# Two gated cross-attention layers: the first layer's maxima in twelve visits of 500 keys in place of sixteen of 375

## Chip, core and metric

The kernel runs on one core of a Trainium2 chip. The metric is the device time of one launch in microseconds (us). A core has five engines with a queue of instructions each, worked off in order: TensorE (PE in the profile, with its weight loads shown as PEld), VectorE (DVE), ScalarE (ACT), GpSimd (POOL) and SyncE (SP), which issues the DMAs here. They wait for each other by semaphores alone. Matmuls write to PSUM, eight banks of 512 fp32 numbers on each partition; DVE and ACT read it.

## What is computed

Eight sequences of 224 rows and 512 columns pass through two layers. Each layer is a cross-attention over 750 context rows and a feed-forward part, each gated by a tanh and added to its input. Layer 0 has 16 heads of 32 numbers, and its feed-forward part quantizes rows and weights and has a convolution of three taps; layer 1 has 8 heads of 64 and an fp4-quantized feed-forward part.

```python
def _L0_xattn_ref(query, key, value, Wq, Wk, Wv, Wo):
    q, k, v = proj(query, Wq), proj(key, Wk), proj(value, Wv)   # 16 heads x 32
    scores = jnp.einsum('bhqd,bhkd->bhqk', q, k) / jnp.sqrt(jnp.float32(DIM_K))
    attn = jax.nn.softmax(scores, axis=-1)
    x = jnp.einsum('bhqk,bhkd->bhqd', attn, v)
    return x.transpose(0, 2, 1, 3).reshape(b, -1, e) @ Wo.T
...
x = x + jnp.tanh(g_xattn[0]) * _L0_xattn_ref(_layernorm(x, axis=-1), ctx_1024, ctx_1024, ...)
x = x + jnp.tanh(g_ffn[0]) * _L0_ffn_ref(_layernorm(x, axis=-1), ...)
x = x + jnp.tanh(g_xattn[1]) * _L1_xattn_ref(_layernorm(x, axis=-1), ctx_1024, mask, ...)
x = x + jnp.tanh(g_ffn[1]) * _L1_ffn_ref(_layernorm(x, axis=-1), ...)
```

## The kernel before

`run` goes through sixteen attentions: n = 0 to 7 are the eight sequences of layer 0 (`attention16`), n = 8 to 15 those of layer 1 (`attention8`). Then comes layer 1's feed-forward part. The change touches `attention16` alone.

`attention16` has two stages. **The first stage finds the maxima.** For each group g of four heads, each tile i of 112 queries and each half c of 375 keys there is one slot, sixteen in all. A slot has four score matmuls (L504), one for each head, on 32 rows of the array each, into two PSUM tiles `sc` of two banks each; the pool `pair` has two such tiles, so the scores of a slot need the exponentials of the slot before to be done. Two DVE reductions (L512) take the negated maxima of two heads each, and four ACT exponentials (L521) read the same scores with these maxima as bias. Their output `shown` is not used; what counts is the sum (`accum_out`). **The second stage makes the products.** Twelve steps, each for a group and two tiles of 125 keys: the maxima are put into the scores by a small matmul (`pick`, L468), the scores are made transposed (L477), exponentiated by two ACT instructions (L620), and multiplied by the values one step later (`products`, L595). Between the stages `stat_rows` (L446, L450, L456) makes the maxima into rows.

In the rest of the time PE does other work, taken in pieces from generators. `fill(us, ...)` emits pieces until that much PE time is used up, `pace(us, ...)` until DVE is that far behind by the kernel's own count (`self.behind`), and `finish` empties a queue. Emission order is the order on every engine. The pieces are: keys of the next sequence (`keys`, L314, four matmuls of 375 columns for a group), its queries (`queries`: statistics L174, rows L184, transposes L196 with copy L197, matmuls L343), values (`value_tile`, L372, four matmuls of 512 columns, for this layer and for layer 1 later), the output product of the sequence before (`project_out`, L417, with its sum on DVE, L428), and layer 0's feed-forward part, called `ffn0`, with its output product `ffn0_out` (L1040).

Three things matter for the order:

- Keys, queries, values and `project_out` use the PSUM pool `m` of two banks, in turn. A bank is free again when it has been copied out: keys (L323), values (L381) and transposed rows (L197) on ACT, `project_out` on DVE. The copies are emitted after the exponentials of their slot, and ACT keeps that order.
- The `ffn0` of sequence n-1 runs beside attention n (`beside`). What is left of it at the end becomes `old`, and is finished in the first slots of attention n+1 (from n = 2 on). Its last part puts a scale in all partitions (`spread`, matmuls L212, copy L215), then quantizes in four pieces (L1026, L1029); `ffn0_out` takes these four pieces, first for the first tile of rows and then for the second.
- `soon`, `early` and `late` are the queues that `fill` takes from: the first values and `project_out`; `ffn0_out` and the other values; keys and queries of the next sequence. `late` goes on in the second stage.

A slot's two calls of `fill` ask for 1.9 and for 1.6 us plus at most 0.5:

Of the kernel before, what the change touches and what calls it, by code (L numbers as in the profile page):

```python
# [27 lines left out]
F32 = mybir.dt.float32  # L28
# [3 lines left out]
AF = mybir.ActivationFunctionType  # L32
ALU = mybir.AluOpType
AX = mybir.AxisListType

B, S, D = 8, 224, 512
M = 750
TP = 112
TF = 128
NF = B * S // TF  # L40
NT = S // TP
KC = D // 128
MH = M // 2
CP = 125
NKT = M // CP
SOON = 4
# [18 lines left out]
class Net:  # L65
# [31 lines left out]
    def setup(self):  # L97
# [207 lines left out]
    def keys(self, n, c, g):  # L305

        nc, job = self.nc, self.jobs[n]
        if "kT" not in job:
            job["kT"] = [
                self.att.tile([128, M], F32, name="kT", bufs=2 * KC) for _ in range(KC)  # L310
            ]
        pk = self.ps("m", [128, MH])
        for k in range(KC):
# [171 lines left out]
    def attention16(self, n, before, ahead, old, soon, early, late, beside):  # L485

        nc, pool, job = self.nc, self.att, self.jobs[n]
        kT, qT = job["kT"], job["qT"]
        rows = [slice(h * 32, (h + 1) * 32) for h in range(4)]


        part = pool.tile([TP, 2, NT, KC, 4], F32, name="part")
        sums = pool.tile([TP, 2, NT, KC, 4], F32, name="sums")
        slots = KC * NT * 2
        self.behind = 1.0
        for slot in range(slots):  # L500
            g, i, c = slot // (2 * NT), slot // 2 % NT, slot % 2
            sc = [self.ps("pair", [TP, 2, 512]) for _ in range(2)]
            for h, r in enumerate(rows):
                nc.tensor.matmul(  # L504
                    sc[h // 2][:, h % 2, :MH],
                    lhsT=qT[r, g, i * TP : (i + 1) * TP],
                    rhs=kT[g][r, c * MH : (c + 1) * MH],
                    start=True,
                    stop=True,
                )  # L510
            for k in range(2):
                nc.vector.tensor_reduce(  # L512
                    part[:, c, i, g, 2 * k : 2 * k + 2], sc[k][:, :, :MH], AX.X, ALU.max, negate=True
                )
            if slot == 0:
                self.finish([before])

                shown = pool.tile([CP, 4, 2 * S], F32, name="p", bufs=2)
            self.put_off()
            for h in range(4):  # L520
                nc.scalar.activation(  # L521
                    shown[:TP, h, :MH],
                    sc[h // 2][:, h % 2, :MH],
                    AF.Exp,
                    bias=part[:, c, i, g, h : h + 1],
                    accum_out=sums[:, c, i, g, h : h + 1],
                )


            self.fill(1.9, soon, early, late)  # L530
            if slot == 3:
                self.finish(soon)
                self.finish(old)
            elif slot < 3:
                self.pace(1.0, old)
            if slot in (10, 11):

                self.behind += next(ahead)[1]
            if (slot > 2 or n == 0) and slot < slots - 1:
                self.pace(1.0, beside)  # L540
            more = min(max(self.behind - 2.3, 0), 0.5)
            self.fill(1.6 + more, soon, early, late)
            self.behind = max(self.behind - 2.3 - more, 0)
        val = pool.tile([TP, NT, KC, 4], F32, name="val")
        nc.vector.tensor_tensor(val, part[:, 0], part[:, 1], ALU.min)
        transposed = self.stat_rows(self.stat[0][n % 2], val.rearrange("p t g h -> p t h g"))
        self.pace(1.0, beside)
        self.fill(1.3, early, late)
        self.finish(early)
        sT = transposed()  # L550
        self.fill(0.7, late)
        self.behind = max(self.behind - 2.5, 0)

        def divisors():

            less = pool.tile([TP, 2, NT, KC, 4], F32, name="less")
            for c in range(2):
                nc.vector.tensor_tensor(less[:, c], val, part[:, c], ALU.subtract)
            nc.scalar.activation(less, less, AF.Exp)
            self.behind += 0.4  # L560
            yield
            nc.vector.tensor_tensor(sums, sums, less, ALU.mult)
            total = pool.tile([TP, NT, KC, 4], F32, name="total0")
            nc.vector.tensor_tensor(total, sums[:, 0], sums[:, 1], ALU.add)
            nc.vector.reciprocal(total, total)
            transposed = self.stat_rows(self.stat_inv, total.rearrange("p t g h -> p t h g"))
            self.behind += 2.2
            yield
            iT = transposed()
            yield  # L570
            for pair in range(2):
                pi = self.ps("t", [128, 2, S])
                for k in range(2):
                    nc.tensor.matmul(
                        pi[:, k, :],
                        lhsT=self.spread_q[:, 2 * pair + k, :],
                        rhs=iT,
                        start=True,
                        stop=True,
                    )  # L580
                across[pair] = pool.tile([128, 2, S], F32, name="inv")
                nc.scalar.copy(across[pair], pi)
                yield

        aT = job["aT"] = pool.tile([128, KC, S], F32, name="aT")
        more, across, banks = divisors(), {}, {}

        def products(g, j0, p):

            if g % 2 == 0 and j0 == 0:  # L590
                banks["pa"] = self.ps("pa", [128, 2, S])
            for j in (j0, j0 + 1):
                for h, r in enumerate(rows):
                    col = g * 128 + h * 32
                    nc.tensor.matmul(  # L595
                        banks["pa"][r, g % 2, :],
                        lhsT=job["v"][j][:, col : col + 32],
                        rhs=p[:, h, (j - j0) * S : (j - j0 + 1) * S],
                        start=j == 0,
                        stop=j == NKT - 1,  # L600
                    )
            if g % 2 and j0 + 2 == NKT:
                nc.vector.tensor_tensor(
                    aT[:, g - 1 : g + 1, :], banks["pa"], across[g // 2], ALU.mult
                )
                self.behind += 0.6

        last = None
        for step in range(KC * NKT // 2):
            g, j0 = divmod(2 * step, NKT)  # L610
            pw = [self.ps("pair", [CP, 2, 512]) for _ in range(2)]
            k = kT[g][:, j0 * CP : (j0 + 2) * CP]
            self.weights_minus_max(
                [(pw[h // 2][:, h % 2, : 2 * S], r, g, qT[:, g, :], k) for h, r in enumerate(rows)],
                self.pick, sT, True,
            )
            p = pool.tile([CP, 4, 2 * S], F32, name="p", bufs=2)
            self.put_off()
            for k in range(2):
                nc.scalar.activation(p[:, 2 * k : 2 * k + 2, :], pw[k][:, :, : 2 * S], AF.Exp)  # L620
# [12 lines left out]
        def rest():  # L633
            products(*last)
            yield 0.8, 0.6

        return rest()
# [939 lines left out]
```

## Time and profile before

| what | us |
|---|---|
| median of three runs (2120.82 to 2123.0) | 2121.07 |
| the profiled execution | 2120.87 |
| its span on the core | 2119.1 |
| PE busy | 2078.0 (98% of the span) |
| DVE busy | 1362.2 (64%) |
| ACT busy | 1005.9 (47%) |
| maxima of sequence 5: first scores at 667.91, second stage from 749.77 | 81.86 |
| second stage of sequence 5: to the next first scores at 798.48 | 48.71 |

The span is that of the core's instructions; 1.8 us of the execution lie outside it. Busy time counts an instruction from its start to its end, and matmuls overlap, so PE can be short of its full pace while it is counted as busy. In a timeline, neighbouring instructions of one line are merged into one row: start, duration, engine, line, operation, tiles, count, and in brackets the engine's idle time just before with what ended it. An fp32 matmul shows as two matmuls.

### The profile page before, as it was taken

The page shows a single profiled execution, that of the slowest core. Times are in us where ns is not written, and L with a number is a line of the kernel's source. Part 1 is how long each engine was busy: PE and PEld are TensorE (multiplying, and loading weights), DVE is VectorE, ACT ScalarE, POOL GpSimd, SP SyncE. Part 2 cuts the span into 40 slices and gives each one's busy share as a digit, 9 for nine tenths or more (in the row PEclk, how much of TensorE's full clock was granted, in tenths as well). Part 3 has the DMA queues.
Part 4 walks back from the last instruction along what each step waited for, and adds up shares of the span by engine and source line. Part 5 has one row for each costly group of instructions (what it writes and reads, how often), then busy time and mean ns, then how long its engine had stood idle before and what let it go on. Part 6 is the DMA issues. An engine that isn't in the chain of part 4 may idle for free.

```text
span 2119.1 us, 32277 instructions
## 1 busy us (share of the span) xinstructions
PE 2078.0 (98%) x12606; PEld 1197.8 (57%) x12606; DVE 1362.2 (64%) x2795; ACT 1005.9 (47%) x2332; POOL 130.3 (6%) x146
## 2 busy tenths in 40 slices
PE   9999999999999999999999999999999999999999
PEld 5454544545445454554657567667666665565555
DVE  3777666575666756657547667767743577676665
ACT  3656656566565665657626444544544321111111
POOL 0000000000000000000000011111100011111111
PEclk9999999999999999999999999999999999999999
DMA  7301001020010201112021122222320020000000
GB/s 249 99 31 44 6 24 44 1 60 7 28 40 1 66 2 32 35 41 67 25 63 38 47 90 62 93 65 69 112 62 19 28 89 11 5 21 20 20 6 20
DMA packets 58536, 97.63 MB, mean 46 GB/s; under 512 B 3664, under 2 KB 30032, under 8 KB 58256
## 3 DMA queue, kind: packets, MB, share of 16 engines
q1 hardware_dynamic: 58384, 95.57, 14.3%
q8 instruction: 100, 1.64, 0.3%
q14 instruction: 52, 0.43, 0.1%
HBM read 73.47 MB, written 22.09 MB: 45 GB/s over the span
## 4 chain that ended last, share of the span: by engine, by line
PE 94%; ACT 3%; DVE 2%; issue 0%; POOL 0%; ACTq 0%; POOLq 0%; DVEq 0%
PE ps_m L372 16%; PE ps_m L314 15%; PE ps_big L1187 11%; PE ps_m L1219 6%; PE ps_m L417 5%; PE ps_pair L504 5%; PE ps_m L343 5%; PE ps_half L722 4%; PE ps_half L782 4%; PE ps_pa L685 4%; PE ps_pair L477 3%; PE ps_pa L595 3%; PE ps_t L926 2%; PE ps_m L1187 2%; ACT p L620 2%; PE ps_pair L468 2%
## 5 line engine op out<-in xcount | busy, mean ns | idle before, releaser
L521 ACT ACTIVATE p<-ps_pair,part 112x375 f32<-112x375 f32 x512 | 286.2, 571 | 204.3 <-DVE part L512 204.3
L314 PE MATMUL ps_m<-cx,wk 128*128 128x375 f32 x1024 | 367.1, 490 | 12.9 <-ACT xnT L197 11.7
L512 DVE TENSOR_REDUCE part<-ps_pair 112x2 f32<-112x750 f32 x256 | 228.3, 933 | 157.0 <-PE ps_pair L504 157.0
L314 PEld LDWEIGHTS ps_m<-cx,wk 128*128 128x128 f32 x1024 | 181.7, 191 | 123.2 <-issue 22.3
L739 DVE CUSTOM_DVE_ANT_0 ps_half<-ps_half,mbias 112x750 f32<-112x750 f32 x128 | 121.1, 946 | 138.4 <-PE ps_half L722 138.4
L620 ACT ACTIVATE p<-ps_pair 125x896 f32<-125x896 f32 x192 | 165.3, 912 | 90.9 <-PE ps_pair L477 90.2
L372 PE MATMUL ps_m<-wv_later,cx 128*125 128x512 f32 x384 | 185.7, 607 | 0.0
L372 PE MATMUL ps_m<-wv,cx 128*125 128x512 f32 x384 | 182.8, 606 | 0.0
L760 ACT ACTIVATE p<-ps_half,nm 112x750 f32<-112x750 f32 x128 | 113.4, 890 | 67.2 <-DVE nm L751 66.9
L1219 PE MATMUL ps_m<-wd,hqT 128*128 128x512 f32 x308 | 136.6, 592 | 0.0
L504 PE MATMUL ps_pair<-kT,qT 32*112 32x375 f32 x1024 | 122.1, 519 | 0.2
L1198 ACT ACTIVATE gth<-ps_big 128x352 f32<-128x352 f32 x48 | 22.2, 463 | 207.2 <-PE ps_big L1187 198.5
L417 PE MATMUL ps_m<-wo,aT 128*112 128x512 f32 x256 | 118.9, 599 | 0.0
L954 DVE SCALAR_TENSOR_TENSOR y<-hp,cw,y 128x224 f32<-128x224 f32 x256 | 109.5, 449 | 6.5 <-ACT y L940 2.0
L372 PEld LDWEIGHTS ps_m<-wv,cx 128*125 128x125 f32 x384 | 66.4, 187 | 82.0 <-issue 80.6
L343 PE MATMUL ps_m<-xnT,wq 128*128 128x224 f32 x512 | 111.5, 359 | 0.6 <-ACT xnT L197 0.6
L1187 PE MATMUL ps_big<-wu,xqT 128*128 128x352 f32 x352 | 111.3, 459 | 0.0
L1187 PE MATMUL ps_big<-wg,xqT 128*128 128x352 f32 x352 | 111.3, 459 | 0.0
L934 DVE TENSOR_TENSOR hp<-ps_t,bc 128x448 f32<-128x448 f32 x64 | 39.9, 623 | 108.8 <-PE ps_t L926 98.1
L787 ACT COPY p<-ps_half 125x672 f32<-125x672 f32 x128 | 85.8, 722 | 49.8 <-PE ps_half L782 49.7
L372 PEld LDWEIGHTS ps_m<-wv_later,cx 128*125 128x125 f32 x384 | 64.7, 187 | 69.3 <-issue 68.5
L521 ACT ACTIVATION_READ_ACCUMULATOR p<-ps_pair,part 112x1 f32 x512 | 103.7, 203 | 0.0
(226 smaller groups left out, 3168.0 us busy)
## 6 DMA issues: line engine op xcount, KB each, us to landing
cx<-in_ctx SPq DMA_DIRECT2D x32, 750.0 KB
wst<-in_w SPq DMA_DIRECT2D x16, 512.0 KB
v_later<-vsome SPq DMA_DIRECT2D x32, 250.0 KB
v<-v_later SPq DMA_DIRECT2D x32, 250.0 KB
x<-in_x SPq DMA_DIRECT2D x8, 448.0 KB
mid<-x SPq DMA_DIRECT2D x8, 448.0 KB
x<-mid SPq DMA_DIRECT2D x8, 448.0 KB
last<-x SPq DMA_DIRECT2D x8, 448.0 KB
```

The costliest lines, as they stand in the source:

```text
L314: nc.tensor.matmul(pk, lhsT=self.w["wk"][:, k, g * 128 : (g + 1) * 128], rhs=job["cx"][c][:, k, :], start=k == 0, stop=k == KC - 1,)
L343: nc.tensor.matmul(pq[:, g - g0, :], lhsT=self.w["wq"][:, k, g * 128 : (g + 1) * 128], rhs=xnT[:, k, :], start=k == 0, stop=k == KC - 1,)
L372: self.nc.tensor.matmul(pv, lhsT=self.jobs[n]["cx"][c][:, k, at : at + CP], rhs=self.w[weight][:, k, :], start=k == 0, stop=k == KC - 1,)
L417: nc.tensor.matmul(po, lhsT=aT[:, g, i * TP : (i + 1) * TP], rhs=self.w["wo"][:, g, :], start=g == 0, stop=g == KC - 1,)
L504: nc.tensor.matmul(sc[h // 2][:, h % 2, :MH], lhsT=qT[r, g, i * TP : (i + 1) * TP], rhs=kT[g][r, c * MH : (c + 1) * MH], start=True, stop= ...
L512: nc.vector.tensor_reduce(part[:, c, i, g, 2 * k : 2 * k + 2], sc[k][:, :, :MH], AX.X, ALU.max, negate=True)
L521: nc.scalar.activation(shown[:TP, h, :MH], sc[h // 2][:, h % 2, :MH], AF.Exp, bias=part[:, c, i, g, h : h + 1], accum_out=sums[:, c, i, g, ...
L620: nc.scalar.activation(p[:, 2 * k : 2 * k + 2, :], pw[k][:, :, : 2 * S], AF.Exp)
L739: nc.vector.tensor_tensor_reduce(out=src, in0=src, in1=masks[i], scale=1.0, scalar=-MASKED, op0=ALU.add, op1=ALU.max, accum_out=mx,)
L760: nc.scalar.activation(p[:, h, :].rearrange("p (c k) -> p c k", c=2), sc[h][:, :, :MH], AF.Exp, bias=nms[h], accum_out=total[:, i, h, g : ...
L1187: nc.tensor.matmul(ps[:, :CW], lhsT=xqT[:, k, :], rhs=wt[:, k, c0 : c0 + CW], start=k == 0, stop=k == KC - 1,)
L1219: nc.tensor.matmul(po, lhsT=hqT[:, k, :], rhs=wd[:, k, :], start=k == 0, stop=k == NC1 - 1)
```

## The change

Each group of heads now has three slots in place of four. The first slot takes keys 0 to 499 for query tile 0. The second takes keys 500 to 749 for tile 0 and keys 0 to 249 for tile 1, side by side in one PSUM bank. The third takes keys 250 to 749 for tile 1. So every slot fills 500 columns of a bank. The middle one has eight score matmuls of 250 columns and eight exponentials of 250; the others have four of 500 each. A slot still has two reductions, over 1000 numbers on each partition in place of 750, and in the middle slot one reduction gives four maxima. `shown` is now one row of 500 numbers that all heads write. `part` and `sums` have their axes in another order, and `val`, `less` and `total0` follow it. With twelve slots the calls between them have other sizes and places: `fill` asks for 1.9 and then 2.5 (middle slot: 3.7) plus at most 0.5, `old` gets `pace(2.0)` in slot 0 and is finished in slot 1 (before: `pace(1.0)` in slots 0 to 2, finished in slot 3), `soon` is finished from slot 2 on, and `beside` gets `pace(1.4)` from slot 2 to 10 (before: 1.0 from slot 4 to 14).

```diff
+WIDE = 500
...
-        part = pool.tile([TP, 2, NT, KC, 4], F32, name="part")
-        sums = pool.tile([TP, 2, NT, KC, 4], F32, name="sums")
-        slots = KC * NT * 2
+        part = pool.tile([TP, NT, 2, KC, 4], F32, name="part")
+        sums = pool.tile([TP, NT, 2, KC, 4], F32, name="sums")
+        parts = part.rearrange("p i c g h -> p (i c) g h")
+        added = sums.rearrange("p i c g h -> p (i c) g h")
+        pieces = (
+            ((0, 0, WIDE),),
+            ((0, WIDE, M), (1, 0, M - WIDE)),
+            ((1, M - WIDE, M),),
+        )
+        slots = KC * len(pieces)
         self.behind = 1.0
         for slot in range(slots):
-            g, i, c = slot // (2 * NT), slot // 2 % NT, slot % 2
+            g, third = divmod(slot, len(pieces))
+            some = pieces[third]
+            width = some[0][2] - some[0][1]
+            two = len(some) == 2
             sc = [self.ps("pair", [TP, 2, 512]) for _ in range(2)]
-            for h, r in enumerate(rows):
-                nc.tensor.matmul(
-                    sc[h // 2][:, h % 2, :MH],
-                    lhsT=qT[r, g, i * TP : (i + 1) * TP],
-                    rhs=kT[g][r, c * MH : (c + 1) * MH],
-                    start=True,
-                    stop=True,
-                )
+            for e, (i, k0, k1) in enumerate(some):
+                for h, r in enumerate(rows):
+                    nc.tensor.matmul(
+                        sc[h // 2][:, h % 2, e * width : (e + 1) * width],
+                        lhsT=qT[r, g, i * TP : (i + 1) * TP],
+                        rhs=kT[g][r, k0:k1],
+                        start=True,
+                        stop=True,
+                    )
+            ats = slice(third + (third == 2), third + (third == 2) + len(some))
             for k in range(2):
                 nc.vector.tensor_reduce(
-                    part[:, c, i, g, 2 * k : 2 * k + 2], sc[k][:, :, :MH], AX.X, ALU.max, negate=True
+                    parts[:, ats, g, 2 * k : 2 * k + 2].rearrange("p e h -> p h e"),
+                    sc[k][:, :, :WIDE].rearrange("p h (e w) -> p h e w", w=width),
+                    AX.X,
+                    ALU.max,
+                    negate=True,
                 )
...
             for h in range(4):
-                nc.scalar.activation(
-                    shown[:TP, h, :MH],
-                    sc[h // 2][:, h % 2, :MH],
-                    AF.Exp,
-                    bias=part[:, c, i, g, h : h + 1],
-                    accum_out=sums[:, c, i, g, h : h + 1],
-                )
+                for e in range(len(some)):
+                    at = ats.start + e
+                    nc.scalar.activation(
+                        shown[:, e * width : (e + 1) * width],
+                        sc[h // 2][:, h % 2, e * width : (e + 1) * width],
+                        AF.Exp,
+                        bias=parts[:, at, g, h : h + 1],
+                        accum_out=added[:, at, g, h : h + 1],
+                    )
             self.fill(1.9, soon, early, late)
-            if slot == 3:
+            if slot == 1:
+                self.finish(old)
+            elif slot == 0:
+                self.pace(2.0, old)
+            else:
                 self.finish(soon)
-                self.finish(old)
-            elif slot < 3:
-                self.pace(1.0, old)
-            if slot in (10, 11):
+            if slot in (7, 8):
                 self.behind += next(ahead)[1]
-            if (slot > 2 or n == 0) and slot < slots - 1:
-                self.pace(1.0, beside)
-            more = min(max(self.behind - 2.3, 0), 0.5)
-            self.fill(1.6 + more, soon, early, late)
-            self.behind = max(self.behind - 2.3 - more, 0)
+            if (slot > 1 or n == 0) and slot < slots - 1:
+                self.pace(1.4, beside)
+            free = 3.6 if two else 2.6
+            more = min(max(self.behind - free, 0), 0.5)
+            self.fill((3.7 if two else 2.5) + more, soon, early, late)
+            self.behind = max(self.behind - free - more, 0)
```

More of the change, by code (lines that the diff above doesn't have):

```diff
@@ L518, in attention16 @@
                 shown = pool.tile([CP, 4, 2 * S], F32, name="p", bufs=2)
+                shown = shown[:TP].rearrange("p h q -> p (h q)")[:, :WIDE]
             self.put_off()
             for h in range(4):
-                nc.scalar.activation(
-                    shown[:TP, h, :MH],
-                    sc[h // 2][:, h % 2, :MH],
-                    AF.Exp,
-                    bias=part[:, c, i, g, h : h + 1],
-                    accum_out=sums[:, c, i, g, h : h + 1],
-                )
-            self.fill(1.9, soon, early, late)
-            if slot == 3:
+                for e in range(len(some)):
[7 more added lines that the diff above has]
+                    )
+            self.fill(1.9, soon, early, late)
+            if slot == 1:
[3 more added lines that the diff above has]
+            else:
                 self.finish(soon)
-                self.finish(old)
-            elif slot < 3:
-                self.pace(1.0, old)
-            if slot in (10, 11):
+            if slot in (7, 8):
                 self.behind += next(ahead)[1]
-            if (slot > 2 or n == 0) and slot < slots - 1:
-                self.pace(1.0, beside)
-            more = min(max(self.behind - 2.3, 0), 0.5)
-            self.fill(1.6 + more, soon, early, late)
-            self.behind = max(self.behind - 2.3 - more, 0)
+            if (slot > 1 or n == 0) and slot < slots - 1:
[4 more added lines that the diff above has]
+            self.behind = max(self.behind - free - more, 0)
         val = pool.tile([TP, NT, KC, 4], F32, name="val")
-        nc.vector.tensor_tensor(val, part[:, 0], part[:, 1], ALU.min)
+        nc.vector.tensor_tensor(val, part[:, :, 0], part[:, :, 1], ALU.min)
         transposed = self.stat_rows(self.stat[0][n % 2], val.rearrange("p t g h -> p t h g"))
@@ L554, in divisors @@
         def divisors():
-            less = pool.tile([TP, 2, NT, KC, 4], F32, name="less")
+            less = pool.tile([TP, NT, 2, KC, 4], F32, name="less")
             for c in range(2):
-                nc.vector.tensor_tensor(less[:, c], val, part[:, c], ALU.subtract)
+                nc.vector.tensor_tensor(less[:, :, c], val, part[:, :, c], ALU.subtract)
             nc.scalar.activation(less, less, AF.Exp)
@@ L563, in divisors @@
             total = pool.tile([TP, NT, KC, 4], F32, name="total0")
-            nc.vector.tensor_tensor(total, sums[:, 0], sums[:, 1], ALU.add)
+            nc.vector.tensor_tensor(total, sums[:, :, 0], sums[:, :, 1], ALU.add)
             nc.vector.reciprocal(total, total)
```

## The prediction

> **What bounds the kernel now.** I read the page first, then the waits, then the timelines of sequence 5 (start, last slot), of the end of sequence 0, and the clock.
>
> ```profile
> PE 2078.0 (98%) x12606; PEld 1197.8 (57%) x12606; DVE 1362.2 (64%) x2795; ACT 1005.9 (47%) x2332; POOL 130.3 (6%) x146
> ...
> L521 ACT ACTIVATE p<-ps_pair,part 112x375 f32<-112x375 f32 x512 | 286.2, 571 | 204.3 <-DVE part L512 204.3
> ...
> L512 DVE TENSOR_REDUCE part<-ps_pair 112x2 f32<-112x750 f32 x256 | 228.3, 933 | 157.0 <-PE ps_pair L504 157.0
> ```
>
> PE sets the time. The reductions are a large group on DVE, but DVE is idle for 36% of the span, so a microsecond saved there is none saved in the end.
>
> ```profile
> 430.15 0.90 PE L504 MATMUL ps_pair<-kT,qT 32*112 32x375 f32 x8
> 430.98 0.29 PEld L372 LDWEIGHTS ps_m<-wv,cx 128*125 128x125 f32 x2 [0.54 <-issue]
> 430.98 3.70 PE L372 MATMUL ps_m<-wv,cx 128*125 128x512 f32 x8
> 431.08 1.78 DVE L512 TENSOR_REDUCE part<-ps_pair 112x2 f32<-112x750 f32 x2 [1.79 <-PE ps_pair L504]
> 431.51 0.19 PEld L372 LDWEIGHTS ps_m<-wv,cx 128*125 128x125 f32 x1 [0.24 <-issue]
> 431.94 0.19 PEld L372 LDWEIGHTS ps_m<-wv,cx 128*125 128x125 f32 x1 [0.24 <-issue]
> ...
> 432.12 0.57 ACT L521 ACTIVATE p<-ps_pair,part 112x375 f32<-112x375 f32 x1 [2.08 <-DVE part L512]
> ...
> 432.68 0.56 ACT L521 ACTIVATE p<-ps_pair,part 112x375 f32<-112x375 f32 x1
> ...
> 434.23 0.21 ACT L521 ACTIVATION_READ_ACCUMULATOR p<-ps_pair,part 112x1 f32 x1
> ```
>
> Rows are start, duration, engine, line. This is one slot of sequence 3. PE goes on with a value tile while the slot's chain runs: scores to reduction 0.93, reduction to first exponential 1.04, exponentials every 0.555, free at 434.44, 4.29 after the scores began. PE's own slot is 4.46. So the chain is hidden by 0.17.
>
> ```profile
> 744.65 0.54 ACT L197 COPY xnT<-ps_m 128x448 f32<-128x448 f32 x1
> ...
> 745.25 0.58 PE L314 MATMUL ps_m<-cx,wk 128*128 128x375 f32 x1 [2.06 <-ACT xnT L197]
> ```
> ```profile
> PE ps_m L314 <- ACT xnT L197: 11.7, 6, 2.1
> ```
>
> The wait that does reach PE: a copy that frees a bank of `m` stands behind the slot's exponentials on ACT. It costs 2.06 in each of six sequences.
>
> ```profile
> 145.88 1.73 ACT L620 ACTIVATE p<-ps_pair 125x896 f32<-125x896 f32 x2 [1.19 <-PE ps_pair L477]
> ...
> 146.85 1.69 PE L504 MATMUL ps_pair<-kT,qT 32*112 32x375 f32 x8
> ```
> ```profile
> 614.30:617.70 3.40, 3.40 (x13) 1.92 (x12) 1.05 (x3) 0.00 (x0) 0.00 (x0) 0.50 0.00 0
> ```
>
> The first shows steps without fill: ACT's two exponentials set the pace (steps start every 2.91), and the next scores take 1.69 in place of 0.90. The second: 0.50 is the granted clock, for 3.4 us after a wait of 2.06.
>
> **The change, part by part.**
>
> *A. Scores on PE: -12.3.* Passes of 512 columns start every 0.43, so a column costs 0.84 ns. A slot's eight matmuls run as two passes (four row tiles at once): 2 x 375 x 0.84 = 0.63. The slot takes 0.83 until the next line starts, 0.09 more before it (last pass of L372 to the scores) and 0.10 in the first pass after it (430.98 to 431.51 in place of 0.43): 1.02, of which 0.39 is entry and exit. A slot of 500 columns is 0.84 + 0.39 = 1.23; the middle slot has four passes of 250, also 0.84, and enters once. Per sequence 16 x 1.02 = 16.3 becomes 12 x 1.23 = 14.8. Eight times 1.53 is 12.3. If each query tile in the middle slot paid entry again (3 x 0.09 over 32 slots = 8.6), 3.7 is left. I take 12.3: the second stage's L477 passes of 224 columns follow each other at 0.19 on the same row tiles.
>
> *B. DVE and ACT: nothing by themselves.* 64 reductions fewer, each with some 0.15 fixed (750 numbers 0.93, L819's 1024 in 1.21, 1.04 ns each), save DVE 9.6, hidden by its idle time; if DVE were the bound that would be the gain. ACT has as many exponentials as before: 256 of 500, 256 of 250. By the rows of 375 (0.571) and 750 (L760, 0.890) they take 0.85 ns a column, so one comes every 0.66 or 0.45. A slot's chain is then 0.93 + 0.21 (two passes, 125 columns more), 1.29 (1000 numbers: 1.19), and 2.8 or 3.75: free 5.2 after the scores began, 6.2 in the middle slot. PE's slot with fill of 4.4 or 5.6 takes 5.6 or 6.8, so the chain itself is still hidden, now by 0.4 to 0.6. Small DVE operations with other strides cost the same.
>
> The Trainium skill ("Perfetto Trace Analysis", Optimizing Scalar/DVE Operations) says grouping helps where the engine is saturated, and where it is not but makes bubbles elsewhere, instructions should be broken up. The rule speaks against this change. By it the sum would be a loss too; it gives no size.
>
> *C. Fill moves out of the second stage: +16.1.* In the built program's order, sequence 5 has 66.4 of fill in the maxima (before 61.7), and 17.1 in the products (21.8). The last three steps have 0.63, 0 and 0.22, where before had 1.7 to 2.0. A filled step takes 2.18 plus its fill (647.62 to 651.32: 3.70 with 1.51). An empty one takes 2.91: +0.73. After an empty last step the next scores wait 0.8 (1.69 in place of 0.90). Sequences 3 to 6: 0.1 + 0.73 + 0.5 + 0.8 = 2.1 each, 8.5. Sequence 7: 1.3. Sequence 0 gets four more empty steps, 2.9; sequence 1 three at part price, 1.6; sequence 2 1.0 + 0.8. (Those after 0 and 1 wait already.) If DVE work kept such steps slow anyway, half: 8; DVE running out of time too (L970 takes 1.73): 20.
>
> *D. `old` in slot 1: +14.0.* In sequences 4 to 7 the whole end of `ffn0` now falls into slot 1. The copy L215 stands behind the eight exponentials: from the slot's scores 6.2, copy 0.36, then four times 1.08 + 0.63 on DVE (rows L1026, L1029), the first ready at 8.3. PE reaches `ffn0_out` after 1.23 + 1.72 + 0.3 + 3.43 = 6.7 and waits 1.6. In slot 2 it waits 0.4 and 0.85 for pieces three and four. Slot 2's reductions are behind all this and L428 on DVE; its exponentials end 0.35 after PE is done: 3.2 a sequence, 12.8. Sequence 3 has L215 earlier, and waits 0.85 + 0.35: 1.2. Before, half of these pieces ran in the last steps and the rest in two slots. If this were hidden: 0.
>
> *E. Banks of `m`: +29.0.* A bank filled in a slot is free at 5.2 (6.2) plus a copy of 0.5 to 0.6, if its copy stands behind that slot's exponentials; its next user comes one tile (4 x 0.86) or one key group (4 x 0.63) after it was filled. Longer slots hold more groups, so this happens more often. An example, sequence 0: slot 0 takes 1.23 + 7 x 0.634 = 5.7. Slot 1 ends a key group in bank two at 5.7 + 1.23 + 0.63 = 7.5 and fills bank one with the next by 10.1; then values want bank two, whose copy stands behind slot 1's exponentials: 5.7 + 6.2 + 0.5 = 12.4, so PE waits 2.3. Through the order in this way, with PE's own times: sequence 0 2.3, 0.3, 1.3, 0.4, 1.9 and 1.7 (slots 1, 2, 4, 7, 8, 10), sum 7.9; sequence 1 0.4, 0.5, 1.6 (7, 8, 11), 2.5; sequence 2 0.4, 1.3, 1.8, 1.3 (4, 7, 10, 11), 4.8; sequences 3 to 7 0.4, 0.8, 0.9, 0.65 (4, 9, 10, 11), 2.75 each, 13.8. Bounds: 0, if each copy came before its slot's exponentials; 60, twice, if each wait put off the next slot's chain.
>
> *F. Waits of before that go: -24.4.* Intervals between scores less 1.02 and fill: 1.0, 3.2, 4.7 for sequences 0 to 2, 3.1 for each later one (2.06 of it the wait shown).
>
> *G. Clock: -1.4.* Two such dips followed a 2.06 wait (sequences 4 and 6: the maxima took 83.3, not 81.9). Without that wait both go; one may return in sequence 0 (2.3). The skill ("TensorE: Matmul & The Clock Gate", Why this matters for your kernels) asks for no idle gap above some 3 us; here 2.06 sufficed. By the page no wait of E would lower the clock, and G would be -2.9.
>
> DMAs: SP's order of loads and stores of `cx`, `x` and `v_later` is the same; the second half of `cx` is asked for 17 us before its keys (19 before), and such a load takes 5 (750 KB at 143 GB/s). POOL has only the small L179, ahead of its need as before. If a load came late, its keys would wait.
>
> Sum: -12.3 + 16.1 + 14.0 + 29.0 - 24.4 - 1.4 = +21.0. Span 2119.1 becomes 2140.1, with 1.8 around it 2141.9; the median of the runs, 2121.07, is 0.2 above the profiled execution. I say **2142**.
>
> **Rivals.**
> 1. *No new bank waits* (E is 0): -8.0, 2113. For: longer slots leave the chain 0.4 to 0.6 of cover, where it had 0.17, and ACT has the same work in all. Against: the 2.06 wait is this very mechanism, and ACT's order shows L323 and L381 behind eight exponentials. It decides from E below 3.8, where the total is faster by over 0.2%.
> 2. *Old is hidden* (D is 0): +7.0, 2128. For: DVE is idle a third of the time. Against: L215 is on ACT, not DVE.
> 3. *The short exponentials do not overlap their accumulator reads.* 0.46 + 0.20 = 0.66 in place of 0.45, eight times 1.7 in 32 middle slots, less their cover of 0.6: +35, 2177. Against: in the slot above, read and next exponential overlap.
> 4. *The change does less than it says.* True of ACT: as many exponentials as before. Already in the sum.
>
> **How the numbers follow.** The forecast has 0.67, rival 1 0.12, rival 2 0.10, rival 3 0.05, something near no change (D and E half, C at 8) 0.06. Two runs of this kernel tell 0.2% (4.2 us) apart. Faster: rival 1, 0.12. Same: 0.08 (the last case and the lower edge of rival 2). Slower: 0.80. The forecast's own range, with C from 8 to 20 and E within a third, is 2125 to 2157. To leave out at most 2 in 10 I go to 2119 below (rival 2 and no change) and 2160 above.
>
> **What would show it.** Right: PE's first L1040 in sequences 4 to 7 waits about 1.6 for DVE; PE rows L314 and L372 with waits for ACT copies of some 30 in all; steps 10 and 11 at 2.9; L504 rows of 1.7 at each sequence's start; the 2.06 wait of xnT gone. A: scores in 1.23 a slot. Wrong: PE waits no longer in sum than now, exponentials of 250 slower than 0.47, or the middle slot's four passes over 1.3.

## The result and the profile after

The changed kernel takes 2153.25 us (median of four runs, 2151.09 to 2153.94), the kernel before 2121.06 in the same series: a ratio of 1.0148, 95% interval 1.013 to 1.0166. It is slower by 32.2 where +21 was forecast. The profiled execution took 2153.94, with a span of 2152.1, 33.0 more than before.

First the busy times of the page after, then its groups with shapes kept apart (line, operation, tiles, count, then busy time and mean ns of one, then the idle time before):

```profile
PE 2081.8 (97%) x12606; PEld 1205.0 (56%) x12606; DVE 1356.5 (63%) x2731; ACT 1016.3 (47%) x2332; POOL 130.5 (6%) x146
```
```profile
L543 ACT ACTIVATE p<-ps_pair,part 112x500 f32<-112x500 f32 x256 | 173.4, 678 | 194.1 <-DVE part L527 187.8
L543 ACT ACTIVATE p<-ps_pair,part 112x250 f32<-112x250 f32 x256 | 116.1, 479 | 78.3 <-DVE part L527 78.3
L543 ACT ACTIVATION_READ_ACCUMULATOR p<-ps_pair,part 112x1 f32 x512 | 104.5, 204 | 0.0
L527 DVE TENSOR_REDUCE part<-ps_pair 112x2 f32<-112x1000 f32 x128 | 147.4, 1193 | 149.9 <-PE ps_pair L518 149.9
```

The operations cost what was forecast: reductions 1.19, exponentials 0.68 and 0.48. DVE's busy time fell by 5.7 and the kernel became slower. The loss must be in PE's waits and its pace. In the new file PE's scores are L518, the copies of keys, values and transposes L324, L382 and L198, and `ffn0_out` is L1064. PE's longest waits after, as total, times and longest:

```profile
PE ps_m L315 <- ACT kT L324: 9.7, 11, 1.6
PE ps_t L1064 <- DVE hs L1053: 9.2, 13, 1.4
PE ps_pair L469 <- ACT p L644: 6.9, 20, 0.4
PE ps_m L197 <- ACT kT L324: 5.9, 7, 1.5
PE ps_m L315 <- ACT xnT L198: 3.2, 2, 1.9
PE ps_m L373 <- ACT v L382: 3.0, 8, 1.1
PE ps_t L213 <- DVE diag L205: 2.4, 2, 1.8
```

The wait of 11.7 for `xnT` is down to 3.2. All waits for banks of `m` (every row on `ps_m` with a copy on ACT, smaller ones included) are some 25, where the kernel before has 15.0, and 9.2 for the quantized pieces are new. This is how both look. PE's timeline of sequence 5, from its first scores to those of slot 3:

```profile
685.78 1.66 PE L518 MATMUL ps_pair<-kT,qT 32*112 32x500 f32 x8
...
693.62 1.11 PE L518 MATMUL ps_pair<-kT,qT 32*112 32x250 f32 x16
694.66 1.97 PE L418 MATMUL ps_m<-wo,aT 128*112 128x512 f32 x4
...
701.85 1.07 PE L1064 MATMUL ps_t<-w,hs 128*112 128x512 bf16 x4 [1.35 <-DVE hs L1053]
702.86 1.11 PE L518 MATMUL ps_pair<-kT,qT 32*112 32x500 f32 x8
703.89 1.07 PE L1064 MATMUL ps_t<-w,hs 128*112 128x512 bf16 x4
705.17 1.07 PE L1064 MATMUL ps_t<-w,hs 128*112 128x512 bf16 x4 [0.21 <-DVE hs L1053]
706.84 1.07 PE L1064 MATMUL ps_t<-w,hs 128*112 128x512 bf16 x4 [0.59 <-DVE hs L1053]
```
```profile
711.29 1.67 PE L518 MATMUL ps_pair<-kT,qT 32*112 32x500 f32 x8
...
711.86 0.27 PEld L518 LDWEIGHTS ps_pair<-kT,qT 32*112 32x112 f32 x4 [0.30 <-ACT p L543]
```

The middle slot's sixteen rows, 250 columns each, take 1.04 to the next line, as do the eight of 500; the eight of 375 took 0.83. `ffn0_out` waits for piece after piece: 2.15 in all. The scores of slots 0 and 3 take 1.60 to the next line: their second half waits for exponentials on ACT, in slot 3 for the late ones of slot 2.

PE and ACT in the middle slot of the last group of sequence 5 (slot 10, counted from 0):

```profile
758.09 1.11 PE L518 MATMUL ps_pair<-kT,qT 32*112 32x250 f32 x16
...
760.53 0.47 ACT L543 ACTIVATE p<-ps_pair,part 112x250 f32<-112x250 f32 x1 [1.80 <-DVE part L527]
...
760.90 0.19 ACT L543 ACTIVATION_READ_ACCUMULATOR p<-ps_pair,part 112x1 f32 x1
760.99 0.46 ACT L543 ACTIVATE p<-ps_pair,part 112x250 f32<-112x250 f32 x1
...
761.90 2.08 PE L315 MATMUL ps_m<-cx,wk 128*128 128x375 f32 x6
...
763.66 0.50 ACT L543 ACTIVATE p<-ps_pair,part 112x250 f32<-112x250 f32 x1
764.01 0.24 ACT L543 ACTIVATION_READ_ACCUMULATOR p<-ps_pair,part 112x1 f32 x1
764.11 0.88 ACT L324 COPY kT<-ps_m 128x375 f32<-128x375 f32 x2
764.67 1.53 PE L315 MATMUL ps_m<-cx,wk 128*128 128x375 f32 x4 [0.69 <-ACT kT L324]
```

The eight exponentials run to 764.1, then the copies of two banks of keys follow together. PE, with both banks full, has waited 0.69 for the first.

The comparison of the two traces by stretches, from one sequence's first scores to the next:

| stretch | before | after | change | forecast |
|---|---|---|---|---|
| to the first scores | 29.23 | 30.76 | +1.5 | 0 |
| sequence 0 | 117.62 | 129.44 | +11.8 | +9.8 |
| 1 | 125.70 | 127.17 | +1.5 | -0.6 |
| 2 | 132.80 | 132.34 | -0.5 | +0.4 |
| 3 | 130.55 | 131.69 | +1.1 | +1.4 |
| 4, 5, 6 | 394.86 | 403.12 | +8.3 | +7.5 |
| 7, and all of layer 1 | 1188.34 | 1197.58 | +9.2 | +2.6 |

The forecast column is the sum of the steps with that sequence, step G's +1.5 put to sequence 0 and its -2.9 to 4 and 6. Sequences 1 to 6 came out within 2.1 in every row. Sequence 5 alone: the maxima grew from 81.86 to 89.98, the products shrank from 48.71 to 44.39, +3.8 together. That the rows of sequences 3 to 6 come so near is in part luck, as the account by steps below shows. The large error is the last row. PE's timeline at the change of layer shows it:

```profile
1088.54 0.43 PE L1029 MATMUL ps_t<-ident,hmx 128*112 128x128 f32 x2
1090.77 0.70 PE L213 MATMUL ps_t<-diag,ones 112*128 112x112 f32 x4 [1.80 <-DVE diag L205]
1091.40 2.84 PE L746 MATMUL ps_half<-kT,qT 64*112 64x375 f32 x8
1094.17 1.26 PE L619 MATMUL ps_pa<-p,v 125*32 125x224 f32 x16
1095.36 1.97 PE L418 MATMUL ps_m<-wo,aT 128*112 128x512 f32 x4
1099.20 1.97 PE L418 MATMUL ps_m<-wo,aT 128*112 128x512 f32 x4 [1.87 <-DVE aT L627]
```
```profile
1091.40:1094.80 3.40, 3.40 (x17) 1.47 (x20) 2.85 (x4) 0.35 (x1) 0.00 (x0) 0.50 0.33 123
```

At n = 7 the kernel finishes what is left of `ffn0` between the last step and layer 1's first scores (L746). PE waits 1.80 for its scale, the clock falls to 0.50 (second fence, a window of the trace: after the busy times of PE, PEld, DVE, ACT and POOL stand the granted clock, the DMA share and GB/s) so that the first scores take 2.84, and the `aT` that `project_out` needs comes late because the four quantizing pieces stand ahead of it on DVE. The second stage of sequence 7 shrank by only 1.8 (48.71 to 46.89) where that of sequence 5 shrank by 4.3, and layer 1's first slot grew from 12.43 to 17.07.

### The profile page after: what moved, and what is told of

Read it like the earlier page. It is cut to its first block, busy times and chain, and to the rows that moved or that the text cites. A ratio compares the mean times of both kernels' runs of the same rounds, so it can differ in the third digit from the quotient of the medians.

```text
span 2152.1 us, 32045 instructions
## 1 busy us (share of the span) xinstructions
PE 2081.8 (97%) x12606; PEld 1205.0 (56%) x12606; DVE 1356.5 (63%) x2731; ACT 1016.3 (47%) x2332; POOL 130.5 (6%) x146
## 4 chain that ended last, share of the span: by engine, by line
PE 83%; ACT 9%; DVE 6%; issue 1%; DMA 0%; SPq 0%; ACTq 0%; POOL 0%; DVEq 0%; POOLq 0%
PE ps_m L373 14%; PE ps_m L315 11%; PE ps_big L1211 11%; PE ps_m L1243 6%; ACT p L543 5%; PE ps_pair L518 5%; PE ps_m L344 4%; PE ps_half L746 4%; PE ps_half L806 4%; PE ps_m L418 4%; PE ps_pa L709 4%; PE ps_pair L478 3%; PE ps_pa L619 3%; DVE part L527 2%; ACT p L644 2%; PE ps_t L950 2%
## 5 line engine op out<-in xcount | busy, mean ns | idle before, releaser
L543 ACT ACTIVATE p<-ps_pair,part 112x250 f32<-112x250 f32 (+1 forms) x512 | 289.5, 578 | 272.3 <-DVE part L527 266.1
L527 DVE TENSOR_REDUCE part<-ps_pair 112x2 f32<-112x1000 f32 (+1 forms) x192 | 221.3, 1194 | 255.1 <-PE ps_pair L518 255.1
L373 PE MATMUL ps_m<-wv_later,cx 128*125 128x512 f32 x384 | 181.2, 603 | 1.4 <-ACT v L382 1.4
L518 PE MATMUL ps_pair<-kT,qT 32*112 32x500 f32 (+1 forms) x1024 | 115.2, 510 | 0.7 <-ACT kT L324 0.6
L806 PEld LDWEIGHTS ps_half<-ident,p 112*125 112x125 f32 x768 | 93.2, 189 | 16.1 <-issue 7.8
```

The costliest lines, as they stand in the source:

```text
L373: self.nc.tensor.matmul(pv, lhsT=self.jobs[n]["cx"][c][:, k, at : at + CP], rhs=self.w[weight][:, k, :], start=k == 0, stop=k == KC - 1,)
L518: nc.tensor.matmul(sc[h // 2][:, h % 2, e * width : (e + 1) * width], lhsT=qT[r, g, i * TP : (i + 1) * TP], rhs=kT[g][r, k0:k1], start=Tru ...
L527: nc.vector.tensor_reduce(parts[:, ats, g, 2 * k : 2 * k + 2].rearrange("p e h -> p h e"), sc[k][:, :, :WIDE].rearrange("p h (e w) -> p h ...
L543: nc.scalar.activation(shown[:, e * width : (e + 1) * width], sc[h // 2][:, h % 2, e * width : (e + 1) * width], AF.Exp, bias=parts[:, at, ...
L806: nc.tensor.transpose(pt[:, j // half, j % half * TP : (j % half + 1) * TP], p[:, h, j * CP : (j + 1) * CP], self.ident[:TP, :TP],)
```

## The experiments

Nine kernels ran in three series. The ratios are against the kernel before, whose median was 2122.18, 2122.10 and 2121.13 in them; differences between kernels of two series carry some 1 us for that.

### 1 to 4: one edit against each of three suspected costs, and all three

The first asks DVE for more of `ffn0` in each slot, so that nothing of it is left over as `old` (against step D):

```diff
-                self.pace(1.4, beside)
+                self.pace(2.4, beside)
```

> The changed kernel, with pace(2.4, beside) in place of pace(1.4, beside) in slots 2 to 10, so that about two pieces of ffn0 go into a slot and its end no longer falls into slot 1 of the next sequence. Theory (the end of ffn0 is late): the wait of the first ffn0_out matmul for DVE's quantizing (9.2 us in all in the changed kernel) falls below 1, slot 1 of sequences 4 to 7 goes from 9.2 to about 7.3 us, the start of layer 1 loses some 5 us, and one more empty step each gives back about 3: 2153 becomes 2138 (2133 to 2143). Rival (reductions of 1000 leave DVE no room in a slot, whatever the order): the pieces put off the reductions instead, each slot grows, 2150 to 2165.

Measured: 2147.94, ratio 1.0119 (1.0103 to 1.0134). 5.3 gained; a miss. The waits of L1064 for the pieces are gone from the list, but a wait of before has come back:

```profile
PE ps_m L315 <- ACT xnT L198: 11.3, 6, 3.2
PE ps_m L315 <- ACT kT L324: 9.9, 8, 1.6
```

By the traces, sequences 0 to 6 and what precedes them took 1.7 more than in the changed kernel; the gain lies behind, in sequence 7 (133.02 instead of 136.88) and layer 1's first slot (13.90 instead of 17.07). But the 1.7 is a balance. Sequences 4 to 6 took about 2 less each, though in each the waits for banks went from 2.6 to 3.5. Sequence 1 took 7.4 more, with a wait of 3.16 for `xnT` and 6.8 us of halved clock.

The second lets the copies of a slot go between its exponentials (against step E):

```diff
-            for h in range(4):
+            def sums_of(heads):
+                for h in heads:
...
+            sums_of((0, 1))
             self.fill(1.9, soon, early, late)
+            sums_of((2, 3))
```

> The changed kernel, with the exponentials of heads 2 and 3 emitted after the slot's first fill, not before it; so copies that free a bank of m are emitted between the two halves, and no copy waits for more than half a slot's exponentials. Theory (copies stand behind the exponentials): PE's waits in L315, L197 and L373 for ACT's copies, 24 us in all, fall below 10, and the clock dips of sequence 0 go; some slots grow by 0.1 to 0.2 since a copy of 0.5 now stands before the last exponentials: 2153 becomes 2136 (2128 to 2143). Rival (the chain scores, reduction, exponentials is what PE waits for): a later end of the exponentials makes it worse, 2156 to 2170.

Measured: 2124.43, ratio 1.0014 (1.0004 to 1.0023): 28.8 gained, more than the expected range. The same slot as above, in this kernel:

```profile
740.25 0.47 ACT L544 ACTIVATE p<-ps_pair,part 112x250 f32<-112x250 f32 x1
740.27 3.34 PE L315 MATMUL ps_m<-cx,wk 128*128 128x375 f32 x10
...
740.70 0.48 ACT L324 COPY kT<-ps_m 128x375 f32<-128x375 f32 x1
741.05 0.50 ACT L544 ACTIVATE p<-ps_pair,part 112x250 f32<-112x250 f32 x1
```

The first copy now stands after four exponentials, and PE's ten keys run without a gap. Of PE's waits on `ps_m` for copies of `kT`, `v` and `xnT`, 5.2 of the 25 are left. The dips of the clock (stretches of 3.41 us at 0.50) went from four to one; at 1.7 each, half of 3.41, that is some 5 of the gain, by estimate.

The third takes some fill out of the maxima, for the last steps of the products (against step C):

```diff
-            if slot in (7, 8):
+            if slot in (8, 9):
...
-            self.fill((3.7 if two else 2.5) + more, soon, early, late)
+            self.fill((3.2 if two else 2.1) + more, soon, early, late)
```

> The changed kernel, with second fills of 2.1 and 3.2 us in place of 2.5 and 3.7 (and the early pieces of the next queries in slots 8 and 9, since the load of the next sequence is emitted later). About 4.5 us of fill a sequence goes back to the second stage. Theory (empty last steps cost 0.7 each, and 0.8 more at the next scores): steps 9 to 11 of sequences 3 to 6 take 2.2 plus fill, gain 2 us a sequence and 14 us in all, less 3 to 5 where the shorter slots no longer cover the chain: 2153 becomes 2143 (2138 to 2150). ffn0's end stays late. Rival (the second stage is paced by ACT or DVE, not by fill): the steps grow by their fill, 2153 to 2160.

Measured: 2170.97, ratio 1.0233 (1.0216 to 1.025). 17.7 lost where 10 were to be gained. (The first line of the edit also moves the early pieces of the next queries by one slot; the two were not tried apart.) The fourth has all three edits:

> The three edits together: ffn0 sooner, copies between the halves of the exponentials, less fill in the first stage. Theory: the three waits are separate, so most of their gains add: 2153 - 15 - 17 - 10 = 2111 (2104 to 2124), below the kernel before (2121) by about the 12 us that PE saves on entering and leaving the score slots. Rival (the waits only move; one chain sets the slot): about the best of the three alone, 2130 to 2140.

Measured: 2101.40, ratio 0.9899 (0.9884 to 0.9913): the fastest of all, 51.9 below the changed kernel and 20.8 below the one before, and 2.6 below the expected range. So the edit that loses 17.7 alone does no harm in company. Why was open.

### 5 and 6: which edit the third one needs

The first two edits without the third, and the last two without the first:

> e2 (copies between the halves of the exponentials) with ffn0 sooner as in e1. In e1 the wait for the quantizing went, but waits for copies came up elsewhere and ate the gain; here copies come early. Theory: now the end of ffn0 shows its own price, 3.2 us in each of four sequences, 1.2 in sequence 3 and some 6 at the start of layer 1, less 3 for more empty steps: from e2's 2124 to 2106 (2102 to 2112). Rival (ffn0's end was never worth more than e1's 5 us): 2119 to 2122.

Measured: 2108.71, ratio 0.9937 (0.9922 to 0.9952), as expected. Less fill then brings 7.3 on top.

> e2 with less fill as in e3. In e3 steps 9 to 11 did become cheap, but two things were added: the copy of the transposed rows stood behind all of slot 11's exponentials, and the end of ffn0 met ffn0_out in slots 1 to 3 with the clock at half. The first goes here, the second stays. Theory (empty steps are worth about 2 us in each of sequences 3 to 7): from e2's 2124 the steps give 10 to 12, the end of ffn0 takes 8 to 12 back: 2122 (2115 to 2130), and in the trace steps 9 to 11 of sequence 5 take 2.2 us plus their fill, and the next scores no longer 1.66. Rival (fill is worth the same in both stages): steps as in e3, but no time gained anywhere else, 2132 or more.

Measured: 2140.49, ratio 1.0084 (1.0067 to 1.0101): far above the range expected, and where the rival had it (2132 or more). With the copies between, less fill still loses 16.1. The timeline of sequence 5's slots 2 and 3 in this kernel, all engines:

```profile
685.35 1.11 PE L518 MATMUL ps_pair<-kT,qT 32*112 32x500 f32 x8
```
```profile
690.22 0.63 DVE L1055 TENSOR_SCALAR hs<-hs 128x896 bf16<-128x896 f32 x1
690.76 1.40 DVE L429 SCALAR_TENSOR_TENSOR x<-ps_m,gate,x 112x512 f32<-112x512 f32 x2
...
692.08 2.30 DVE L527 TENSOR_REDUCE part<-ps_pair 112x2 f32<-112x1000 f32 x2
693.37 0.68 ACT L544 ACTIVATE p<-ps_pair,part 112x500 f32<-112x500 f32 x1 [9.29 <-DVE part L527]
...
694.99 1.09 PE L518 MATMUL ps_pair<-kT,qT 32*112 32x500 f32 x4 [1.29 <-ACT p L544]
```

Slot 2's scores are done at 686.4, but DVE has the quantizing pieces and the sum L429 ahead of their reductions, which start at 692.08. So the exponentials are late, the `pair` banks stay taken, and slot 3's scores wait for them, 1.29 and then 0.51. The list has 8.3 of this wait in ten places, and the clock dips six times. With less fill an `ffn0` that isn't brought forward meets less PE work in slots 1 to 3 to hide behind. In sequence 5 slots 2 and 3 take 9.64 and 9.57 (7.92 in sequence 4, where the clock does not dip); slot 1, with `old` emitted in it, 7.67. With copies between alone they took 8.44, 6.94 and 9.24.

As much is lost in slot 11, 10.90 in place of 8.44. The transposes of the next queries now come just after its scores, so that the copy of `xnT` stands behind two of its exponentials. This is sequence 4:

```profile
612.69 0.60 PE L197 MATMUL ps_m<-ident,xn 112*128 112x112 f32 x4
...
615.55 0.52 ACT L198 COPY xnT<-ps_m 128x448 f32<-128x448 f32 x1
...
616.13 3.42 PE L315 MATMUL ps_m<-cx,wk 128*128 128x375 f32 x10 [1.56 <-ACT xnT L198]
```

In experiment 3 it stands behind all four, and the wait is 3.16 in each of sequences 3 to 7.

### 7: the kernel before with its copies between

```diff
+            sums_of((0, 1))
             self.fill(1.9, soon, early, late)
+            sums_of((2, 3))
```

> The kernel before, with its sixteen slots, and the exponentials of heads 2 and 3 emitted after the slot's first fill as in e2. It tells how much of e4's gain is the wider slots' own. Theory: the wait of 2.06 us in six sequences goes, 11.7, and two clock dips, 2.9; slots have only 0.17 of cover, so some grow by 0.1 to 0.3: 2122 becomes 2110 (2106 to 2117), and e4 stays ahead of it by some 9, nearly the 12 that PE saves with twelve slots. Rival (copies between are all that e4 gained, twelve slots are worth nothing): 2098 to 2104.

Measured: 2118.53, ratio 0.9982 (0.9973 to 0.9992): a little above the range expected, and far from the rival. The `xnT` wait fell from 11.7 to 4.8, but sequence 5 takes 130.52 against 130.57. Single slots went from 4.72 to 5.08 and from 5.53 to 5.91, all of it in their own scores (0.83 to 1.20 and 1.12 to 1.50 until the next line), which wait for the exponentials of the slot before: the narrow slots have 0.17 of cover, and a copy of 0.58 within the chain used it up. What is left of the gain is about two dips of the clock fewer (one in place of three). The fastest kernel with twelve slots is 17.1 below this one (2118.5 to 2101.4), where step A alone is 12.3. That is not the worth of the slots alone: its calls for `ffn0` and for fill were changed too, and sixteen slots with other calls were not tried. With the calls of the changed kernel, twelve slots with the copies between (2124.4) are 5.9 slower than this kernel.

### 8 and 9: the change of layer, and the last combination

The larger call for `ffn0` in sequence 7 alone:

```diff
-                self.pace(1.4, beside)
+                self.pace(2.4 if n == 7 else 1.4, beside)
```

> The changed kernel with the larger call for ffn0 (2.4 in place of 1.4) in sequence 7 alone; sequences 0 to 6 are as in the changed kernel. My theory: the loss at the change of layer comes from the rest of ffn0 that is left over at the end of sequence 7, and nearly all that the larger call gained in every sequence (5.3 by the medians) came from there. In that run sequence 7 and the first slot of layer 1 together took 7.0 less than in the changed kernel, while the seven sequences before took 1.7 more. So here: 2153.25 - 7.0 = 2146 (2144 to 2149), and the 1.8 wait for diag at the change of layer gone. Rival, that step D was of the size forecast in sequences 4 to 7 (3.2 each): sequence 7 alone brings 3, so 2150. If the leftover has nothing to do with the change of layer: 2153.

Measured: 2149.63 (2145.63 to 2156.61), ratio 1.0139 (1.0118 to 1.0159). The time can't tell the theory from the rival. By the trace, it took 3.2 less than the changed kernel from sequence 7's first scores to the end of layer 1's first slot, not 7.0. That is the rival's size, but gained where the theory had it, at the change of layer. The second stage took 43.97 in place of 46.89 and layer 1's first slot 13.90 in place of 17.07: 6.1 gained there, and the wait of 1.80 for `diag` gone. But the maxima took 92.90 in place of 89.99, by a new wait in slot 10:

```profile
1031.34 4.90 PE L315 MATMUL ps_m<-cx,wk 128*128 128x375 f32 x10 [2.94 <-ACT xnT L198]
```
```profile
1031.00:1034.40 3.40, 3.06 (x5) 1.84 (x6) 0.63 (x1) 1.14 (x3) 0.00 (x0) 0.51 0.00 0
```

My 7.0 had counted sequence 7's whole gain in experiment 1, though its `old` comes from sequence 6, which this kernel leaves as it was.

The larger call and less fill, copies behind all exponentials:

> The changed kernel with the larger call for ffn0 and the smaller fill, the exponentials undivided: the last of the eight combinations. My theory: less fill loses 17.7 alone because the quantizing pieces crowd slots 1 to 3, and gains 7.3 once ffn0 is sooner and the copies go between. With ffn0 sooner and the copies still behind all exponentials, the crowding is gone but the bank waits stay (they cost 39.2 between the kernel with the larger call alone, 2147.9, and that with the copies between as well, 2108.7): 2147.9 - 7.3 = 2141 (2134 to 2148). Rival, that less fill needs the copies between and not the sooner ffn0: it stays slower than the larger call alone, 2155 or more.

Measured: 2126.78 (2122.46 to 2128.22), ratio 1.002 (1.0012 to 1.0029): 21.2 below the larger call alone. Both numbers were wrong, the rival's the wrong way round: less fill needs the sooner `ffn0`, and doesn't need the copies between. It even brings more without them: sequences 3 to 6 take 130.25 each, where those of experiment 1 took 132.2 to 132.5, with no dip of the clock in either. With this all eight combinations are there:

| | fill as changed | less fill | less fill brings |
|---|---|---|---|
| the changed kernel | 2153.25 | 2170.97 | +17.7 |
| `ffn0` sooner | 2147.94 | 2126.78 | -21.2 |
| copies between | 2124.43 | 2140.49 | +16.1 |
| both | 2108.71 | 2101.40 | -7.3 |

Copies between bring 25.4 to 39.2 in every pair, `ffn0` sooner from 5.3 to 44.2. The larger numbers of `ffn0` sooner, 39.1 and 44.2, belong to the kernels with less fill, where the leftover `ffn0` has least to hide behind.

Much of what less fill costs is the clock. In the profiled executions it dips four times in the changed kernel and thirteen times with less fill alone, once and six times with the copies between. At 1.7 each that is some 15 of the 17.7 and 8.5 of the 16.1, by estimate; the mean granted clock of all four runs with less fill alone, 0.987 to 0.990 against 0.997 to 0.998, says the same. With both other edits there is no dip, with and without less fill. The number of dips varies between executions: the profiled one of the last kernel has one dip and took 2122.68, 4.1 below the median.

## Why the prediction was right in direction and 12 short

- **A, scores on PE, -12.3.** Confirmed in its parts: 1.04 from scores to the next line, in wide and in middle slots alike, where 0.83 plus 0.21 was the working, and the same 0.09 and 0.10 around them.
- **B, DVE and ACT nothing by themselves.** Confirmed: 1.193 per reduction, 0.678 and 0.479 per exponential. Exponentials of 250 start every 0.44 to 0.46 (760.53 and 760.99 in the slot shown), so they overlap the accumulator reads of 0.20, and rival 3 is out.
- **C, fill out of the second stage, +16.1.** Right in kind: after nearly empty last steps the scores take 1.66 (1.69 said). In sequences 3 to 6 it was oversized. In sequence 5 the step without fill took 2.38, not 2.91, and the one after it 3.15 with 0.22 of fill: 0.95 more than 2.18 each and that fill. The late scores cost 0.56 (1.60 in place of 1.04), not 0.8: 1.5 together in place of 2.1. **The term that failed is "Sequence 7: 1.3".** It priced empty steps and no more; D priced the end of `ffn0` in slot 1 of sequences 4 to 7, and the end that falls after sequence 7 has no such slot. What the fewer and emptier steps leave over there is the whole end of `ffn0`, and it falls between two layers with nothing to cover it: 2.5 more in the second stage than in sequence 5 (46.89 against 44.39) and 4.65 in layer 1's first slot. Experiment 8 shows that cause: with `ffn0` sooner in that one sequence 6.1 of it go, though 2.9 come back as a wait in the maxima.
- **D, `old` in slot 1, +14.0.** Right in place and mechanism, and somewhat oversized: PE's first L1064 of sequence 5 waits 1.35 (1.6 said), all three 2.15 in place of 2.85, and the list has 9.2 in all. Slot 2's late exponentials, 0.35 in the working, cost 0.56 in slot 3's scores (1.60 in place of 1.04). Together 2.7 in place of 3.2. With the copies between, the larger call shortened sequences 4 to 6 by 3.4 to 3.7 each (131.7 to 128.0 and 128.3); what else it moved is in that number.
- **E, banks of `m`, +29.0.** Right: some 25 of waits. From 700 to 960, two sequences' time, they are 5.2 where 5.5 was said; in sequences 0 and 1 7.3 in place of 10.4. 28.8 came back with copies between: some 20 in these waits, some 5 by the clock, and some 4 that are not accounted for. Rival 1, which had none of these waits, is refuted.
- **F, waits of before, -24.4.** The wait of 2.06 for `xnT` is gone from sequences 3 to 7. (The 11.7 are five of 2.06 and one of 1.38 in sequence 2, not six of 2.06.) Sequence 5's other waits before were 0.73 for `inv` and 0.33 for `sT` in the second stage, with the 2.06 3.1 in all; 0.42 and 0.20 of them are left.
- **G, clock, -1.4.** Wrong in sign. Three dips before (614.3, 877.1, 1102.4, of which the step counted two), four after (43.5, 98.1, 241.5, 1091.4), +1.7 instead. Two of the four lie in sequence 0, one in 1, where the step allowed for one in all. The dips are most of what sequences 0 and 1 took beyond the forecast, and how many there are is partly chance: experiment 8, with the same code there, has one of the three, and these sequences took 127.75 and 125.73, 1.7 and 1.4 less.
- Rival 2, `old` hidden, is refuted by the 9.2. The start of the kernel gave 1.5 that no step had. The first scores wait 0.56 for a copy of `kT`, because keys 0 to 499 need the second half's copy too. Another 0.9 is a wait of PE for the DMA of `wk`, which isn't the change's: it is 1.3 in experiment 7, with the slots of before, and missing in experiment 5, with the new ones.

With the sizes measured here sequence 5 would have grown by 2.8: A -1.5, C +1.5, D +2.7, E +2.6, F -2.5. It grew by 3.8, near the 3.4 forecast. So 1.0 has no step, and terms that were too large made up for it: that is the luck in the rows of sequences 3 to 6.

Of the 12.0 that were missing in the span, 6.6 lie in the last row of the table, most of it at the change of layer, 4.1 in sequences 0 and 1, where the dips are, and 1.5 at the start.

The Trainium skill ("Perfetto Trace Analysis", Optimizing Scalar/DVE Operations) says that breaking instructions up may help where ACT or DVE isn't saturated but holds up another engine. No run here tests that by itself, since no instruction was split. Opening the order of four or eight for a copy points the same way: 28.8 came back.

## What to carry to other kernels

Fewer and larger batches save PE's entry cost, but on an engine that works in order each copy queued behind a longer batch frees its bank later: emit the copies in the middle of the batch. That needs slack in the batch's own chain: with the narrow slots it brought only 3.6. When the number of visits changes, everything that is metered by visits (side work, fill, what is left over at the end of a loop) must be metered anew, and the place where the last visit's leftover falls must be looked at by itself. Edits that each remove a visible wait don't add up: one lost 17.7 alone and gained 21.2 beside another, so try them in pairs before throwing one away.

## What the runs showed of the hardware

Around some short waits of PE the granted clock falls to 0.50 for 3.41 us: one of 1.80 at the change of layer, one of 2.94 in experiment 8, and before two of the five of 2.06. It doesn't follow always: three of those five didn't bring it, and a wait of 2.19 at 97 us was followed by it in the changed kernel and not in experiment 8, whose code is the same there. The Trainium skill ("TensorE: Matmul & The Clock Gate", Why this matters for your kernels) names a gap above some 3 us as what to avoid; here these waits were shorter, and the measurement decides. An exponential with a sum takes 479, 571 and 678 ns for 250, 375 and 500 columns: the first 250 cost far more than the next.
